# Low halves of the attention context made by adding transfers issued from GpSimd, in a perceiver block on one core

## The chip, the core and the metric

The kernel runs on one core of a Trainium2 chip. A core has a matrix engine (TensorE, called PE in the profile, with its weight loads under PEld), three elementwise engines (VectorE as DVE, ScalarE as ACT, GpSimd as POOL), a queue that issues the loads (SyncE as SP), and sixteen DMA engines behind the queues. The metric is the device time of one execution in microseconds. The kernel before took 231.92 us (median of 3 runs, 229.8 to 232.12).

## The reference

Two batch elements of 128 rows and 512 columns pass through three blocks, each added to `x`: a block of self-attention, cross-attention over a context of 2048 rows per batch element and a feed-forward; a recurrent block over two steps (the two batch elements); and an attention with selected experts. The change touches the first block:

```python
def self_attn(x, Wq, Wk, Wv):
    Q, K, V = (x @ Wq, x @ Wk, x @ Wv)
    energy = jnp.einsum('bqd,bkd->bqk', Q, K)      # masked by length and causally
    score = jax.nn.softmax(energy / np.sqrt(DK), axis=-1)
    return jnp.einsum('bqk,bkd->bqd', score, V)

def cross_attn(x, context, Wq, Wk, Wv):
    Q = x @ Wq
    K, V = (context @ Wk, context @ Wv)
    energy = jnp.einsum('bqd,bkd->bqk', Q, K)      # masked by length
    score = jax.nn.softmax(energy / np.sqrt(DK), axis=-1)
    return jnp.einsum('bqk,bkd->bqd', score, V)

z = self_attn(x, Wq1, Wk1, Wv1)
x = layer_norm(x + z, ln1_g, ln1_b)
z = cross_attn(x, context, Wq2, Wk2, Wv2)
x = layer_norm(x + z, ln2_g, ln2_b)
z = jax.nn.relu(x @ fc1_w + fc1_b) @ fc2_w + fc2_b
return layer_norm(x + z, ln3_g, ln3_b)
```

All inputs are float32. The kernel multiplies in another order: the scores are (x Wq2 Wk2^T) times the context, and the probabilities are multiplied with the context itself before Wv2.

## The kernel before

**Two ways to multiply.** A product of float32 operands is one call of the matrix engine that the profile shows as two matmul records. In the other way an operand is cut into a high half, rounded to the type fp32r, and a low half, what the rounding left over; the product is then three matmuls (high by high, high by low, low by high), one record each. The class `Halves` holds such a pair. `evac(dst, src)` makes it: ACT copies (CAST) into `dst.hi`, and DVE subtracts (TENSOR_TENSOR) `src - hi` into `dst.lo`.

**The context.** Each of the two batch elements (`t` = 0, 1) has its context in four groups `g` of 512 rows, twice: transposed (`ctxT`, tiles `cT`, for the scores) and as it is (`ctx`, tiles `cN`, for the products with the probabilities). A group is one load of 1 MB into a tile of 4 chunks. `load_ctxT` cuts all eight `cT` groups into halves. `load_ctxN` cuts only the groups in `PCR`, which are 0 and 1 of each batch element; groups 2 and 3 stay float32. I write cN02 for the group of `t` = 0, `g` = 2, and so on. `cross_attention` makes the scores of a group with 12 matmuls of 128x512, then counts, masks and takes the maximum (tiles `em`, `mx`, `nmax`, on DVE), the four exponentials (ACT, `em<-em,nmax`), turns each group of probabilities around on the matrix engine, copies it out of PSUM (`pT`), and adds the product with the context into one bank: 12 matmuls for a cut group, 4 for a whole one. The sum leaves as tile `PC`.

**Before the cross-attention.** `queries` normalises x, turns it (`hT`, halves) and multiplies with Wq1, Wk1, Wv1, each loaded in four chunks of 128 rows that `load_w` cuts into halves. `cross_queries` multiplies the turned result of the self-attention (`u1T`, float32) with Wq2 for both batch elements at once (128x256), and the result, in halves, with Wk2T.

**Memory.** Tiles of 8 KB per partition come from a pool with tag `wide` (8 of them, for loads and float32 weights) and a pool with tag `hl` (4 pairs, for halves). A tile's first writer waits until the last reader of the tile that had the place is done. The parameters, banks and small tiles have pools of their own.

**Order.** Nothing runs when the functions are called: `Program` and `Engine` number every operation in the order of the calls (line 172), and `emit(ORDER)` (line 158) issues them in an order written out by hand or by a tool, as numbers and runs such as `257+7`. Each engine takes its own instructions strictly in that order; an instruction that waits holds up all behind it on its engine. That is why all groups of the profile stand at line 161. In the kernel before the cross-attention's first exponential has number 642; just ahead of it on ACT stand the four copies of cN00.

Of the kernel before, what the change touches and what calls it, by code (L numbers as in the profile page):

```python
# [16 lines left out]
P = 128  # L17
# [25 lines left out]
257+7 0 249 1 250+1 4 2 275 7 252 3 276 20 17 26 423 277+1 23 253+2 35 38 256 29 32 279 281 18 280 265+4 10 271 21 272  # L43
283+1 446 19 285 22 291+1 282 293+1 317 287 24 27 273 288 286 270 295+1 318+2 289 25 28 321 274 297+2 322+1 290 300+3
324+1 30 304+1 33 306+2 343 309+2 326+1 312 328 313 44 344 39 36 329+3 31 345 333+1 34 335 346+4 314 40 37 336+2 351+5
339 357+9 340 88+1 424 41 5 369+7 45+1 90 42 57 367 91 377+10 315 43 50 11 388+4 316 95 395 426 409+2 368 464+1 396
412 427 92 8 341 47 51 393 413 115 52 394 342 414 48+1 61 466 397 62 467 398+1 415 468 9 428+1 400 430 469 431 63 401
473 432+1 470 93 435 434 416 471 67 417 58 472 418 402+1 436+4 419 474+1 420+1 476 404+2 441 477+1 94 96 442 407 443
79 484 444 408 445 479 447+2 481 422 450+1 480 53 485 482 486 483 487+1 453 452 454 489 455 490 492+1 491 496+1 68 456
494+1 458+1 64 498 457 80 86 461 499 460 81+1 84 87 85 59+1 54 65+1 69 83 120 70 122 121 116 512 502 513 503 514 504+3  # L50
515 508+1 516 510 517 550+1 518+1 522+2 552+1 525 511 526 554 520 527+1 555 529 556+1 521 558 530 559+2 531+1 562 118
533 563 534+2 564 537+3 123 541+2 565+1 544 567 545 119 500 568+2 546 117 571+2 547 604+3 71 608 574 609+3 578 613 501
73 72 575 591 614 97 548 759 615 579 77 74 78 133 576 75+1 580 592 581+1 593 583 577 584+2 594 587 616 98 588+1 617
595 102 549 103 596+1 154 100 99 598 618 599+1 619 104 101 620+1 106 138 136 12 601+1 134 105 785+1 622+3 16 139 425
183 137 590 626+1 142 140 135 107 787 628 788+4 746 109 747 603 124 141 760 108 761+1 110 629 113 630 111 15 13+1 198
631 112 125 127 632 763 793 764+5 748+1 770 750 128 639 637 129 131 635 640 55 772+1 126 774+1 794 776 795 751+1 777+2
633 753 796 638 157 646 636 159 161 634 155 641 130 642 651+1 754 653 643 654 780 114 755 669+1 756 132 655 657 671+1
163 166 174 156 781 658 757 158 656 645 659+1 782 661+2 783 160 164 673 664+1 162 666+1 165 668 167 674+1 644 687 676
696 677 688 697 689 678+1 168+1 680+2 690 56 170 784 698 683 699 758 173 186 171 771 797 172 190 175 177 188 798+1
684+2 691+1 145 181 146 179 800 178 693+2 803 700 807 801 805 143 804 808 701+2 802 806 809+1 819+2 180 811 144 822+1  # L60
704 825 176 837+1 826 705 707 824 827 708 828+2 706 711+1 839 831 184 709 715 812 840 832+1 813 147 238 182 716 185
864 717 865+1 834+2 841 843 867 814 189 199 187 844 842 718 710 855+1 719 857+1 720 713 194 815+2 845+5 151+1 200 193
148 647 149 648+1 721 851+1 722 191 150 723 153 724 192 714 859 725 462+1 213+1 868 853+1 726 743 195+1 215+1 860+2
217 197 225 219 863 650 727 869 729 870 730 728 731+1 218 871+1 733+2 226 937 739+1 220 240 221 736 204 873 227 874+2
879 737 877 234 880 913 925 883+1 878 738 914 885+1 881 887 741 915 742 882 888 916 889 917 890+1 990 205 744+1 206
235+1 892+1 918 894 201 818 202 926 895 897 896 898+1 919+4 927+5 934 900 924 203 938+3 933 209 942+1 935 231 901+1
944+2 903 936 911 947 904 912 905 948+1 210 950 906 952 951 907+1 910 978 909 232 979 966+4 228+1 971+2 980+2 974
983+1 975+1 985 987 986 988 991 953+3 992+2 957 960 958 961 959 962 977 995 963+2 222 996 989 997+2 1019 223 1020+1
1000 1022+1 1001+1 1179 1024 1029 1025 1031 230 1026 233 1005 1037+2 1003 1006 1076 1004 1084 1098 1030 1108 1099
1040+1 1102 1007 1027 212 1100 1032 1109 1078 1103 1085+1 1035 1033 239 1116 1110 1042 1120 1043 1101 1111 1044 1008+1  # L70
1013 1010 1014 1011+1 1015+1 237 1077 1017 1034 1117 1082 1119 224 1148 1018 1226 1045 1118 1036 1046 1151 1149+1 1228
1080 1227 1083 1047+1 1079 1087 1229+1 211 1054 1051 1231 1236 1232+2 1121 1088 1125+2 1104 1237 1105 1122+1 207 1050
1081 1112 1333 1313 1335 1089+5 1315 1314 1316+1 1290 1334 1332 1336 1343 1337 1095 1338 1344 1128 1339 1289 1287+1
208 1053 1055 1106 1056 1113 1291 1107 1292+1 1052 1049 1124 1096+1 1238 1355 1057 1129 1114+1 1356 1130 1132 1294+2
1345 1239 1065 1241 1062 1400 1028 1346 1297+3 1318 1340 1325 1301+1 1319 1326 1320+1 1240 1242 1133 1341 1354 1402
1401 1303+2 1243+1 1403 1327 1245+1 1328 1247 1353 1357 1071 1248 1347 6 1058+1 1131 1358+1 1363 1360 1364+2 1068 1361
1157 1249+7 1404 1060 1134 1061 1069 1342 1063+1 1322 1074 1306+1 1066 1073 1144 1308 1067 1158 1152+1 1070 1309 1142
1329 1351 1072 1348 1138 1154+1 1352 1075 1310 1141 1349 1139 1330 1145 1140 1136+1 1159+1 1198 1135 1367 1362 1146
1323 1331 1324 1147 1350 1173 1260 1259 1143 1311 1368 1162 1387 1370 1163 1263 1261 1371 1264 1262 1164 1156 1369
1258 243 1257 1161 1265 1269 1165 1267 1167+1 1405 1266 241 1268 1166 1271 1170+1 1406 1169 1273 1172 1372 245 1270  # L80
1378 1272 1388 1312 1384 1389 1278 1174+1 1276 1176 1180 1177 1181 1206 1182+1 1410+1 1385+1 1407 1412+1 1408 1390
1379 1277 1284 1281 1374 1391 1382 1280 1282 1285 1275 1392 1178 1286 1377 1279 1283 1394 1373 246 1376 1393 1184 1380
1395 1383 1375 1185 1396 1186+1 1397+1 1381 242 1188+1 244 1190+6 1207+2 248 1274 1197 1414 1409 1399 1415 1417 1416
1418+1 1210 1420 1199+3 1211 1429 1212 1421 1423 1422 1203 1213 1426 1204 1427+1 1424+1 1205 1214+2 1220 1217 1221
1218 1222 1219 1223+1 1454 1430+1 1435 1432+1 1436+2 1225 1483 1482 1439 1485+1 1484 1462 1487+2 1523 1532 1434 1440+2
1533 1490 1534 1443 1497+2 1444+3 1524 1450 1506 1500 1235 1448 1455 1451 1449 1453 1463 1452 1456 1464 1457 1465 1458
1466 1459+1 1467+1 1461 1469+3 1501+2 1491 1476 1473 1477 1474+1 1492 1507+1 1504 1535 1525 1478+1 1493 1526 1494 1509
1536 1510+1 1527+1 1537+1 1529 1512 1530 1539 1495 1480+1 1516 1612 1611 1496 1613+1 1521 1513 1617 1615 1505 1517
1531 1549 1540 1514 1550+2 1515 1569 1518 1570 1519 1571+1 1616 1618 1652 1620 1653 1621 1619 1622+1 1520 1522 1543
1553 1556 1554 1654 1562 1557 1555 1563 1661+4 1655 1545 1573 1577 1541+1 1574 1576 1635 1656+1 1575 1579 1582 1658+1  # L90
1636 1580 1559+1 1666 1544 1624 247 1625 1637 1626+2 1564 1629+1 1667 1638 1668 1650 1558 1583 1631+1 1581 1584 1639
1633 1660 1546 1640+2 1645 1644 1669 1646+1 1634 1643 1678+2 1561 1681 1578 1648 1698 1592 1699+1 1649 1651 1547 1672
1589 1673 1701 1670+1 1548 1585+3 1675+1 1682 1674 1683 1688 1565 1684 1686 1685 1689 1691+1 1702+1 1690 1677 1566
1687 1593 1567 1693 1718 1694+2 1704 1697 1705+1 1719 1708 1707 1709 1711+1 1710 1568 1714+1 1713 1716+1 1742+2 1733
1724+1 1720 1726+1 1721 1728+1 1722+1 1730 1734 1731 1735+1 1594 1745 1737+1 1732 1751 1746 1739+1 1747 1590+1 1741
1748 1756 1752 1595+1 1749 1597 1757 1598 1750 1599+1 1758 1753+1 1759+1 1755 1601 1606 1602+1 1607+1 1604+1 1609+1
"""
OPT = set("""psc fc2 Wv Wk u2col bfpe z4pe z1pe q2 hhcol""".split())

ON_ACT = [set("vsum vc vv bv".split()), set("vsum vc vv bv".split())]  # L100
PCR = [{0,1},{0,1}]
WHOLE = set("Wv1 Wv2 fc2 Wv Wk".split())
VPE = set()
WIDE_W = set("Wq1 Wk1".split())
NDUM, TDUM, HLB, WDB, UNS = 10, 0, 4, 8, 0


class Halves:
# [69 lines left out]
def perceiver_kernel(ctx: ExitStack, tc: tile.TileContext, a: dict, out: bass.AP):  # L178
# [81 lines left out]
    onemu = const.tile([P, 6 * KC], F32, name="onemu")  # L260


    def load(kind, dst, src):
        with program.on(kind):
            sync.dma_start(dst, src)

    class Rows:


        def __init__(self, name, n):  # L270
            self.tiles = []
            for i in range(0, n, 4):
# [13 lines left out]
    def load_w(name, n=C, rows=C):  # L286
# [13 lines left out]
        for k in range(kc):  # L300
            w = big.tile([P, C], F32, tag="stage", name=f"w_{name}", bufs=3) if whole is None else whole[:, k, :]
            load("s", w[:, :n], a[name][k * P : (k + 1) * P, :])
            with program.on("w"):
                evac(hl[:, k, :n], w[:, :n])
# [836 lines left out]
```

## Time and profile before

| | |
|---|---|
| median of 3 runs | 231.92 us (229.8 to 232.12) |
| the profiled execution | 230.57 us, of which the span of its instructions is 228.8 us |
| PE / DVE / ACT / POOL busy | 218.0 / 186.9 / 136.1 / 17.4 us |
| mean granted TensorE clock | 0.985 of full speed |
| moved by DMA | 43.41 MB, 190 GB/s on average |
| queries and self-attention | from the start to about 36 us |
| Wq2, Wk2T | 37.1 to 50.0 us |
| scores and products of the cross-attention | first scores at 49.98, last `PC` copy from 105.03 us |
| feed-forward, recurrent block, expert attention | from there to the end |

The page gives, for the most expensive groups of instructions, busy time, the mean duration of one, and what the engine waited for ahead of them. Consecutive instructions of an engine overlap a little at their ends, so what one costs in a row of them is the distance of the starts, which is worked out from the timeline: a row of n instructions that lasts L with a single duration d costs (L - d)/(n - 1) each. A matmul record of a float32 product is half of the product.

### The profile page before, as it was taken

Reading aid. Unit: us, or ns where it says so; the run is one execution under the profiler, and the core shown is the slowest. Engines: PE = TensorE matmul, PEld = TensorE weight load, DVE = VectorE, ACT = ScalarE, POOL = GpSimd, SP = SyncE. Lnnn points to the kernel's source line nnn. Section 1 sums busy time; section 2 is a strip of 40 time slices with the busy share of each in tenths; the row PEclk is TensorE's granted clock in tenths of the full one; section 3 lists DMA queues with packets and bytes.
Section 4 is the critical chain, followed back from the end, with each engine's and each line's share of the span. In section 5 each row is a group of like instructions: output and inputs, shape, how many; then the busy total and the mean of one; then the engine's idle time right before and its main releaser. Section 6 shows DMA issues by size and latency. Waiting matters only on the chain.

```text
span 228.8 us, 3607 instructions
## 1 busy us (share of the span) xinstructions
PE 218.0 (95%) x1186; PEld 179.8 (79%) x1186; DVE 186.9 (82%) x456; ACT 136.1 (59%) x418; POOL 17.4 (8%) x39
## 2 busy tenths in 40 slices
PE   7699997999999999999999999999999999998993
PEld 6499865898877846846898888888777978897992
DVE  4674588879999999978999769999997289999822
ACT  2766366727849939446569899988552316437020
POOL 3200001000000000001112200030302020000000
PEclk9999999999999999999999999999999999997699
DMA  5999799999653986858789600684050000000002
GB/s 178 329 393 335 235 370 392 320 322 341 201 221 116 365 299 218 315 151 327 264 294 409 239 0 3 197 288 158 0 209 0 0 1 3 0 1 3 0 0 92
DMA packets 21897, 43.41 MB, mean 190 GB/s; under 512 B 1283, under 2 KB 2871, under 8 KB 21879
## 3 DMA queue, kind: packets, MB, share of 16 engines
q1 hardware_dynamic: 21808, 43.16, 54.0%
q8 instruction: 9, 0.15, 0.3%
q14 instruction: 9, 0.07, 0.1%
q10 hardware_dynamic: 71, 0.03, 0.0%
HBM read 42.66 MB, written 0.52 MB: 189 GB/s over the span
## 4 chain that ended last, share of the span: by engine, by line
PE 58%; DVE 27%; ACT 5%; POOL 4%; DMA 2%; issue 2%; SPq 1%; DVEq 0%; POOLq 0%; ACTq 0%
PE bank L161 58%; DVE ve L161 4%; DVE st L161 3%; POOL rinv L161 2%; DMA w_Wq<-in_Wq_dram 2%; DVE Y L161 2%; DVE pr L161 2%; POOL rs L161 2%; ACT mix L161 2%; DVE X L161 1%; DVE nb L161 1%; DVE v L161 1%; SPq L161 1%; DVE mixhl L161 1%; DVE kn L161 1%
## 5 line engine op out<-in xcount | busy, mean ns | idle before, releaser
L161 DVE TENSOR_TENSOR hl_ctxT<-cT,hl_ctxT 128x512 fp32r<-128x512 f32 x32 | 20.8, 681 | 2.2 <-ACT hl_ctxT L161 2.1
L161 POOL TENSOR_TENSOR rinv<-ve,nhalf 128x1 f32<-128x1 f32 x16 | 10.6, 662 | 149.9 <-DVE ve L161 138.9
L161 ACT CAST hl_ctxT<-cT 128x512 fp32r<-128x512 f32 x32 | 18.2, 622 | 4.3 <-PE bank L161 2.5
L161 PE MATMUL bank<-hl_ctxT,qkTh 128*128 128x512 f32 x64 | 18.4, 394 | 0.0
L161 PE MATMUL bank<-cN,pT 128*128 128x512 f32 x32 | 14.5, 595 | 0.0
L161 PEld LDWEIGHTS bank<-hl_ctxT,qkTh 128*128 128x128 f32 x64 | 11.9, 188 | 2.3
L161 PE MATMUL bank<-hl_ctxN,pTh 128*128 128x512 f32 x32 | 11.9, 420 | 0.0
L161 DVE TENSOR_TENSOR hl_Wv<-w_Wv,hl_Wv 128x512 fp32r<-128x512 f32 x12 | 8.2, 688 | 4.1 <-ACT hl_Wv L161 4.1
L161 PE MATMUL bank<-hl_ctxT,qkTl 128*128 128x512 f32 x32 | 11.2, 396 | 0.0
L161 ACT CAST hl_ctxN<-cN 128x512 fp32r<-128x512 f32 x16 | 9.0, 619 | 3.1 <-PE bank L161 3.1
L161 PEld LDWEIGHTS bank<-cN,pT 128*128 128x128 f32 x32 | 5.9, 190 | 5.9 <-issue 5.7
L161 DVE TENSOR_TENSOR hl_ctxN<-cN,hl_ctxN 128x512 fp32r<-128x512 f32 x16 | 10.4, 681 | 0.0
L161 ACT CAST hl_Wv<-w_Wv 128x512 fp32r<-128x512 f32 x12 | 7.4, 625 | 4.7 <-DVE spread L161 3.4
L161 PE MATMUL bank<-xnT,w_fWk 128*128 128x128 f32 x64 | 9.8, 276 | 0.0
L161 PEld LDWEIGHTS bank<-xnT,w_fWk 128*128 128x128 f32 x64 | 8.7, 192 | 0.9
L161 PE MATMUL bank<-hT,hl_Wq 128*128 128x256 f32 x48 | 7.7, 293 | 1.8 <-ACT hT L161 1.8
L161 PE MATMUL bank<-xnT,w_fWq 128*128 128x128 f32 x64 | 9.3, 275 | 0.0
L161 PEld LDWEIGHTS bank<-xnT,w_fWq 128*128 128x128 f32 x64 | 8.4, 192 | 0.6
L161 PEld LDWEIGHTS bank<-u2T,w_fc 128*128 128x128 f32 x64 | 8.3, 191 | 0.7 <-ACT u2T L161 0.2
L161 PE MATMUL bank<-u2T,w_fc 128*128 128x128 f32 x64 | 8.8, 280 | 0.0
L161 PEld LDWEIGHTS bank<-hT,hl_Wq 128*128 128x128 f32 x48 | 6.5, 190 | 2.7 <-ACT hT L161 2.4
L161 PE MATMUL bank<-w_Wa,mix 128*128 128x256 f32 x32 | 8.5, 379 | 0.0
(282 smaller groups left out, 611.4 us busy)
## 6 DMA issues: line engine op xcount, KB each, us to landing
cT<-in_ctxT_dram SPq DMA_DIRECT2D x8, 1024.0 KB, 8.0
cN<-in_ctx_dram SPq DMA_DIRECT2D x8, 1024.0 KB, 5.5
spread<-in_spread_dram SPq DMA_DIRECT2D x9, 512.0 KB, 6.5
w_Wv<-in_Wv_dram SPq DMA_DIRECT2D x12, 256.0 KB, 3.5
w_Wk<-in_Wk_dram SPq DMA_DIRECT2D x8, 256.0 KB, 5.0
w_Wq<-in_Wq_dram SPq DMA_DIRECT2D x4, 256.0 KB, 4.6
w_Wq<-in_Wq_dram SPq DMA_DIRECT2D x1, 1024.0 KB, 9.4
w_Wk2T<-in_Wk2T_dram SPq DMA_DIRECT2D x4, 256.0 KB, 2.7
```

Source lines behind the costliest of these rows:

```text
L161: self.tc.keep_in_program_order(op(*args, **kwargs))
```

## The change

- `ACC = {"ctxN"}`: where a context group for the products is cut, DVE no longer makes the low half. ACT makes the high half as before, and also writes the negated high half into the place of the low one (`act.mul(..., -1.0)`, rounded to fp32r as well). Then one transfer from SBUF to SBUF, issued from GpSimd's queue, adds the float32 group onto it. Per group: 8 ACT instructions and 1 transfer of 1 MB in place of 4 ACT and 4 DVE instructions.
- `PCR` goes from groups {0,1} and {0,1} to {0,1,2} and {0,1,2,3}: 7 of 8 groups are cut instead of 4. Only cN03 stays float32.
- `MIX = {"Wq1": 1}`: the first chunk of Wq1 is not cut. It is multiplied as float32 with a float32 copy of the first chunk of the turned x (`hF`, two extra ACT copies); the other three chunks as before.
- `q2row`: the product with Wq2 is made for one batch element at a time (128x128 instead of 128x256, twice as many).
- One pool: halves are two tiles of the tag `wide`, which has 16 places; the tag `hl` is gone.
- The two small loads of `turn_rows` move from ACT's queue into the numbered program, on SP.
- `TAILW` adds matmuls that keep the matrix engine busy at the end; all its counts are 0, so it adds none.
- A new `ORDER`. The number of an operation changes where operations are added ahead of it: the load of cN02 is now 174, its four high halves 175, 177, 179, 181, its four negated copies 176, 178, 180, 182, its adding transfer 183, and the first exponential is 687. The load of cN00 is 154, of cN01 164, of cN11 195; the tile cT11 is loaded by 115 and cut by 116 to 123.

```diff
-OPT = set("""psc fc2 Wv Wk u2col bfpe z4pe z1pe q2 hhcol""".split())
+OPT = set("""psc fc2 Wv Wk u2col bfpe z4pe z1pe q2 hhcol q2row""".split())
-PCR = [{0,1},{0,1}]
+PCR = [{0,1,2},{0,1,2,3}]
+MIX = {"Wq1": 1}
+ACC = {"ctxN"}
+TAILW = (0, 0, 0)
-    big = ctx.enter_context(tc.tile_pool(name="big", bufs=8))
+    big = ctx.enter_context(tc.tile_pool(name="big", bufs=16))
...
     def halves(name):
-        hl = big.tile([P, 2, KC, C], F32R, tag="hl", name=f"hl_{name}", bufs=4)
-        return Halves(hl[:, 0], hl[:, 1])
+        return Halves(*(big.tile([P, KC, C], F32R, tag="wide", name=f"hl_{name}") for _ in range(2)))
+
+    def cut(hl, w, n, acc):
+        for k in range(n):
+            if acc:
+                act.copy(hl.hi[:, k, :], w[:, k, :])
+                act.mul(hl.lo[:, k, :], w[:, k, :], -1.0)
+            else:
+                evac(hl[:, k, :], w[:, k, :])
+        if acc:
+            pool.dma_start(hl.lo, w, accum_op=ALU.add)
...
             load("s", w[:, :n], a[name][k * P : (k + 1) * P, :])
+            if k < MIX.get(name, 0):
+                continue
             with program.on("w"):
                 evac(hl[:, k, :n], w[:, :n])
+        if name in MIX:
+            W[name, "whole"] = whole
...
+                m = slice((j + i) * P, (j + i + 1) * P)
+                for kc in range(nw):
+                    pe.matmul(po[:, i, :], whole[:, kc, m], xF[:, kc, :], start=kc == 0, stop=False)
+                matmuls(po[:, i, :], [(w[:, kc, m], xT[:, kc, :]) for kc in range(nw, KC)], False, begun=nw > 0)
...
                 ctxN[t, g] = hl = halves("ctxN")
                 with program.on("w"):
-                    for j in range(4):
-                        evac(hl[:, j, :], c[:, j, :])
+                    cut(hl, c, KC, "ctxN" in ACC)
...
-            for m, po in project_turned(u1T, W["Wq2"], T * P):
-                evac(qT[:, m, :], po)
+            if "q2row" in OPT:
+                for t in range(T):
+                    for m, po in project_turned(u1T[:, :, token(t)], W["Wq2"]):
+                        evac(qT[:, m, token(t)], po)
```

The part of the new `ORDER` around the cutting of cN02 and the first exponential:

```diff
+155 168 121 166 123 170 12 14 172 13 681 15 165 194 167 683 163 803 820 850 804 821+1 805 823 806 824 807 174 180 173
+178 195 679 686 176 808 182 838 851 175 825 809+3 687 696+2 16 852+1 690 750 688 699+1 751+2 714 689 701 715 205 854
```

## Prediction

> **What bounds it.** I read the page's busy line and the chain first.
>
> ```profile
> span 228.8 us, 3607 instructions
> PE 218.0 (95%) x1186; PEld 179.8 (79%) x1186; DVE 186.9 (82%) x456; ACT 136.1 (59%) x418; POOL 17.4 (8%) x39
> ...
> PE 58%; DVE 27%; ACT 5%; POOL 4%; DMA 2%; issue 2%; SPq 1%; DVEq 0%; POOLq 0%; ACTq 0%
> ```
>
> The matrix engine is busy 218.0 of 228.8 us, so work taken from it is worth its time, and any hole made in it costs its length. Next, the ten-microsecond stretches of the cross-attention (busy time of PE, PEld, DVE, ACT, POOL; clock; DMA share; GB/s):
>
> ```profile
> 50.00:60.00 10.00, 10.00 (x47) 8.26 (x46) 9.90 (x21) 7.64 (x16) 0.00 (x0) 1.00 0.76 271
> 60.00:70.00 10.00, 10.00 (x45) 8.09 (x44) 9.90 (x28) 6.58 (x13) 0.00 (x0) 1.00 0.63 224
> 70.00:80.00 10.00, 10.00 (x52) 7.83 (x52) 9.97 (x22) 9.49 (x22) 0.00 (x0) 1.00 0.79 272
> 80.00:90.00 10.00, 10.00 (x37) 5.12 (x35) 9.24 (x23) 6.05 (x15) 0.00 (x0) 1.00 0.66 238
> 90.00:100.00 10.00, 10.00 (x46) 7.38 (x45) 8.72 (x22) 5.79 (x14) 0.00 (x0) 1.00 0.76 280
> ```
>
> PE has no hole, DVE almost none, ACT has a third free. The change loads the free one. Unit prices come from rows without a hole in the timeline (start, length, engine, what, count, idle before):
>
> ```profile
> 62.49 1.75 PE L161 MATMUL bank<-hl_ctxT,qkTh 128*128 128x512 f32 x7
> 81.12 5.42 PE L161 MATMUL bank<-cN,pT 128*128 128x512 f32 x12
> 37.14 6.31 PE L161 MATMUL bank<-u1T,w_Wq 128*128 128x256 f32 x28
> 115.88 3.99 PE L161 MATMUL bank<-u2T,w_fc 128*128 128x128 f32 x32
> 19.12 3.04 PE L161 MATMUL bank<-hT,hl_Wk 128*128 128x256 f32 x24
> 35.64 1.56 PE L161 MATMUL bank<-ident,x 128*128 128x128 f32 x8 [1.86 <-DVE x L161]
> 74.94 3.74 ACT L161 CAST hl_ctxN<-cN 128x512 fp32r<-128x512 f32 x7
> 90.25 1.28 DVE L161 TENSOR_TENSOR hl_ctxN<-cN,hl_ctxN 128x512 fp32r<-128x512 f32 x2
> ```
>
> With the single durations of the groups (0.39, 0.59, 0.38, 0.27, 0.28; ACT 0.62; DVE 0.68) a halved 128x512 matmul costs 0.227 us, a float32 record 0.439 (a product has two), float32 at 256 columns 0.220, at 128 columns 0.120, halved at 256 columns 0.120, an ACT copy 0.52, a DVE subtraction 0.60.
>
> **Part by part.** *Three more groups cut:* 12 products of 0.878 become 36 matmuls of 0.227: 10.5 to 8.2, PE gains 2.3 us, all on the path. DVE gets three more subtractions for the probabilities, 1.8, but loses sixteen for cN, 9.6.
>
> *Negated copies:* ACT makes 56 copies for cN instead of 16, 40 x 0.52 = 20.8 us more. I take the multiplying copy at the plain copy's price; at the distance of the exponentials (0.73 with their sum) it would be up to 0.2 x 28 = 5.6 more. From the last copy of the combined queries (x Wq2 Wk2T, about the first scores) the new order gives ACT until the `PC` of the second batch element: 13 copies for cT and 52 for cN (33.8), 8 exponentials (5.8), 8 copies of probabilities at 0.49 (3.9), 7 weight copies (3.6), small ones 2.6: 49.7 us. PE has in this stage 96 score matmuls (21.8), 84 halved products (19.1), 8 float32 records (3.5), 12 for Wv2 (2.7), some 5 of turning and first fc1: 52. ACT goes from two thirds to 95% of the stage. It fits only if it never waits.
>
> *It waits.* In a pool of n places I give the k-th tile of `ORDER` (by first write) the place that is freed as number k - n (by last read). That this holds is shown by the kernel before: the pair of cN00 is the 13th of 4 places and gets the 9th freed, the first cT group of the second batch element that the scores are done with, and ACT stood for it:
>
> ```profile
> 67.30 2.19 ACT L161 CAST hl_ctxN<-cN 128x512 fp32r<-128x512 f32 x4 [3.11 <-PE bank L161]
> ```
>
> In the one pool of 16, cN02 is the 45th tile and gets the place freed as 29th: cT11, whose last reader is DVE's subtraction 123. Counting from the first scores, s = 49.98 in this trace, DVE has ahead of it, itself included, 19 subtractions (11.4), 4 counts (2.4), length and masks (2.1), one maximum (0.6), two query halves (1.0): 17.5 without a wait. But cT11 and cT13 are themselves loaded into places that Wk2T and the first scores free, at s and s+3, 5 us before they land, and the low half of cT10 gets a place when the third group's scores end, at s+9; such waits make it up to 21. On SP the load of cN02 stands behind cN01 alone, which is early. It then takes 5.1 at least:
>
> ```profile
> cN<-in_ctx_dram SPq DMA_DIRECT2D x8, 1024.0 KB, 5.5
> ...
> DMA to landing us min/median/max: 5.1/5.5/14.4
> ```
>
> so cN02 is there at s+22.6 to s+26. ACT has come to it by s+20 and holds up all behind it. Its copies 180, 178, 176, 182, 175 stand ahead of exponential 687 there: five, 2.6 us. The first exponential begins at s+25.2 to s+28.7; in the trace before it began at 69.71, s+19.7, on the maximum alone. After it come two more, the copy of the probabilities and its low half, 3.3, then the first product, at s+28.5 to s+32. PE is through its 96 scores at s+22 and has 12 transposes, 1.5, so it stands 5 to 8.4 us. What follows is 29 us for PE and 31 for ACT from the first exponential (29 copies for cN 15.1, weights 3.6, the rest above), so the second `PC` comes at s+57 to s+61 against 105.03 - 49.98 = s+55: 2 to 6 later, the 2.3 already spent. I take 4.
>
> *Transfers.* No row shows an adding transfer. It reads two tiles and writes one, so from below it is a plain 1 MB load, 5.1 to landing; from above the slowest such load, 14.4. I take about 8, nearer the median. Between the last negated copy and the first use the new order leaves 10 to 11 us for cN01, cN02, cN11, cN12, cN13: it decides above that. On the engines, 43.16 MB took 54% of the span, 2.9 us per MB; seven transfers at once or twice that are 20 to 40 us, while 50 to 100 us has 14 free (the DMA column). The overflow of 6 to 26 us moves loads back; the weights of the recurrent block can take it (130 to 140 us has a DMA share of 0.01), the groups of the context can't, so I put it into the rival of late transfers. The Trainium skill, "DMA: Bandwidth & Descriptors", Rules for kernel authors, says the same against the change: another issuing queue gives no bandwidth, all run on the same 16 engines. Its section on the anatomy of one DMA fits 2.0 us plus bytes/436e3, an estimate of 4.4 for 1 MB from GpSimd; by it the transfers would never be late, and the sum would be the one above. On GpSimd's queue the normalisation `x0 rinv` stands behind the transfer of cN13, which waits for ACT's copies; it is early by some 5 us.
>
> *Front.* Wq2 by row: 64 x 0.120 = 7.7 for 32 x 0.220 = 7.0, +0.7; the 1.86 us hole ahead of the turned x shrinks, as the second element's work can lie under Wq2 of the first: I leave 0.5, so -1.4. First chunk whole: 8 x 0.220 for 12 x 0.120, +0.3; one copy (0.52) leaves the start, two of 128x128 come in: 0. Sum -0.4, from -0.9 to +1. `turn_rows`: needed late, 0; on SP it stands behind cT00, two issues of 0.4 us. The pool by itself: as many bytes as before, 0 beyond the waits above; `TAILW`: 0.
>
> *Behind.* Nine weight chunks are still to be cut after the second `PC` instead of six: three subtractions, 1.8, where DVE is busy 0.96 and 0.91 of the two stretches from 110 us. 0 to 1.8; I take 0.8.
>
> Sum: 230.57 (this execution) + 4 - 0.4 + 0.8 = **235.0**. The profiled execution lies 1.35 below the median 231.92, within the spread of the runs (1%), about what a measurement can tell from no change.
>
> **Rivals.** *Faster:* the place of cN02 is free sooner than by my count. To leave no hole the first exponential must begin by s+20.3, so cN02 must land by s+17.7 and be issued by s+12.6. Then PE's 2.3 stays gained, with up to 0.9 in front: 227.4 to 229.6, say 228. For it speaks that DVE is relieved by 7.8 and that ACT's sum fits; against it the order on ACT and the load's 5.1. At the end 5 us ran at half clock (210 to 215); another order could give 2.5 either way. *Transfers late:* if they take 14.4 instead of 10, each batch element's first tight group costs 4.4 more: 235 + 8.8 = 244. *Nothing:* DVE's relief is worth nothing since PE is the bound, ACT's waits eat PE's 2.3: 231.
>
> **Numbers.** Forecast 0.52 (232.5 to 239.4: 2 to 6, front up to +1, behind up to 1.8), late transfers 0.12 (239.4 to 248), faster 0.27 (226.5 to 229.6), nothing 0.09 (229.6 to 232.5). Range 227 to 241, leaving out about 0.05 below and 0.08 above. Faster by over 1% (below 229.6): 0.27; slower (above 234.2): 0.12 and 0.43 of the forecast, 0.55; within: 0.18.
>
> **What would show it.** Right: a hole in PE of 5 us or more just ahead of the first products with the context, ACT waiting there for the load of cN02, DVE well under 9 in the stretches from 50 to 100, 84 halved and 8 float32 records. Wrong: the first exponential within 21 us of the first scores and no hole; or adding transfers landing later than 10 us after their issue, with waits on them; or a Wq2 stage that still begins behind a hole of 1.9 us.

## The result, and the profile after

The changed kernel takes **257.98 us** (median of 4 runs, 255.63 to 259.67), the kernel before on the same chip 230.86 (228.34 to 232.12): a ratio of 1.123, 95% interval 1.105 to 1.141. The forecast was 235.0, with a range up to 241. The direction was right and the size was not: 27 us are lost where 4 were expected. (Some executions of every kernel show a lower granted clock and are over 1.5% longer; ratios here, and times and ratios of the experiments below, leave these out, and the number of runs left is given where it is one or two; the changed kernel then takes 257.3.)

The page of the changed kernel first: busy times, two rows of the 40 slices, the two DMA queues that matter (q1 carries the loads, q0 what GpSimd issues), and the chain that ended last by engine.

```profile
span 253.7 us, 3743 instructions
...
PE 221.5 (87%) x1226; PEld 186.8 (74%) x1226; DVE 180.4 (71%) x444; ACT 156.4 (62%) x461; POOL 23.1 (9%) x46
...
PEclk9999999999995589997968999999999999999799
DMA  6989972999399999999994889992000000000002
...
q1 hardware_dynamic: 21879, 43.19, 47.6%
q0 software_dynamic: 1008, 7.34, 14.4%
...
PE 58%; DMA 18%; DVE 11%; ACT 7%; issue 2%; POOL 1%; SPq 1%; POOLq 0%; ACTq 0%; DVEq 0%
```

PE is no longer busy 95% of the span but 87%. The chain holds 18% DMA where it held 2%. The DMA row is full (9) in all slices but one from 44 to 133 us, which before it was not, and the clock falls to a half in two slices. The seven adding transfers moved 7.34 MB and took 14.4% of the engines' 253.7 us, 36.5 us: 5.2 us of all sixteen engines for one transfer of 1 MB. The loads took 120.8 us for 43.19 MB, 2.8 per MB. **An added megabyte costs the engines nearly twice a loaded one.**

The same stretches that the prediction showed, with the later ones (busy time of PE, PEld, DVE, ACT, POOL; clock; DMA share; GB/s):

```profile
70.00:80.00 10.00, 3.45 (x16) 2.52 (x14) 4.50 (x17) 0.28 (x1) 0.52 (x2) 0.85 1.01 227
80.00:90.00 10.00, 3.79 (x15) 3.17 (x16) 1.43 (x3) 7.18 (x17) 0.87 (x1) 0.50 1.03 357
...
110.00:120.00 10.00, 6.48 (x24) 4.59 (x23) 5.65 (x13) 4.96 (x10) 0.56 (x1) 0.90 1.04 236
120.00:130.00 10.00, 4.88 (x20) 3.17 (x19) 1.08 (x2) 1.73 (x4) 0.00 (x0) 0.84 1.03 386
```

There are two holes, 70 to 90 and 110 to 130 us, and in both every engine but the DMA engines is idle for a part. What ACT and PE wait for is seen in their timelines (start, length, engine, operation, idle before and what ended it):

```profile
69.15 1.12 ACT L166 CAST hl_ctxN<-cN 128x512 fp32r<-128x512 f32 x2
82.75 2.19 ACT L166 ACTIVATE hl_ctxN<-cN 128x512 fp32r<-128x512 f32 x4 [12.47 <-DMA cN<-in_ctx_dram]
...
85.35 0.72 ACT L166 ACTIVATE em<-em,nmax 128x512 f32<-128x512 f32 x1
...
128.27 1.14 ACT L166 CAST hl_fc<-w_fc 128x512 fp32r<-128x512 f32 x2 [13.31 <-DMA w_fc<-in_fc_dram]
```

```profile
86.21 2.46 PE L166 MATMUL bank<-ident,em 128*128 128x128 f32 x10 [12.77 <-ACT em L166]
...
129.82 1.22 PE L166 MATMUL bank<-u2T,w_fc 128*128 128x128 f32 x4 [4.09 <-ACT u2T L166]
```

The first hole is the one of the prediction: ACT stands for the load of cN02, with the first exponential queued behind its copies, and PE stands for the exponential. But it is 12.8 us long, not 5 to 8, and it lies ahead of the turning of the probabilities, since that needs the exponentials. The second was not in the prediction: ACT stands 13.3 us for a chunk of fc2, whose load was issued at 109.78 us and took 18.5, and behind it are the turned `u2T` and the second `PC`. Three more waits of PE between the two are for adding transfers themselves: 0.87, 2.65 and 1.03 us, for cN11, cN12 and cN13.

Where the 25.06 us between the two profiled executions (255.63 and 230.57) come from:

| stretch | before | after | difference |
|---|---|---|---|
| start to first scores | 49.98 | 47.60 | -2.4 |
| first scores to second `PC` | 55.05 | 83.90 | +28.85 |
| second `PC` to the end of the span | 123.8 | 122.2 | -1.6 |
| outside the span | 1.77 | 1.93 | +0.2 |

In the middle stretch PE was busy all of its 55.05 us before. Now it is busy 59.52 of 83.90 and stands 24.38, which is the sum of seven waits: 1.80 and 1.17 (behind cT groups that landed late), 12.77, the three of the transfers, and 4.09. Its busy time is not 2.3 shorter but 4.5 longer. Some 1.1 of that is work that has only moved: six records of products with `u2T` and two more transposes of `x` stand ahead of the second `PC` (6 x 0.12 + 2 x 0.18), and the next stretch lacks them. The rest has two reasons in the same rows, which I have not separated: the clock, 0.88 on average here against 1.00, and rows of matmuls broken up by waits, in which each counts its whole duration.

What the DMA engines did while cN02 was on its way (67.8, its issue, to 82.7; packets, MB, share of the engines, then the landing time of the loads issued in that window):

```profile
q0 software_dynamic: 288, 2.10, 75.2%
q1 hardware_dynamic: 718, 1.44, 27.3%
...
cN<-in_ctx_dram SPq DMA_DIRECT2D x4, 1024.0 KB, 14.9
```

Two adding transfers, those of cN00 (issued at 66.43) and cN01 (69.54), took three quarters of the engines' time in this window; 1.44 MB of loads had the rest (cN02 and a part of what was issued behind it). cN02 was issued at s + 20.2 (s is the time of the first scores), inside the s + 17.5 to 21 of the prediction, and landed 14.9 us later, where the prediction took 5.1.

### The profile page after: what moved, and what is told of

The parts are those of the page before. It is cut to its first block, busy times and chain, and to the rows that moved or that the text cites. A ratio compares the mean times of both kernels' runs of the same rounds, so it can differ in the third digit from the quotient of the medians.

```text
span 253.7 us, 3743 instructions
## 1 busy us (share of the span) xinstructions
PE 221.5 (87%) x1226; PEld 186.8 (74%) x1226; DVE 180.4 (71%) x444; ACT 156.4 (62%) x461; POOL 23.1 (9%) x46
## 3 DMA queue, kind: packets, MB, share of 16 engines
q1 hardware_dynamic: 21879, 43.19, 47.6%
q0 software_dynamic: 1008, 7.34, 14.4%
## 4 chain that ended last, share of the span: by engine, by line
PE 58%; DMA 18%; DVE 11%; ACT 7%; issue 2%; POOL 1%; SPq 1%; POOLq 0%; ACTq 0%; DVEq 0%
PE bank L166 58%; DMA w_fc<-in_fc_dram 7%; DMA cN<-in_ctx_dram 6%; DMA cT<-in_ctxT_dram 4%; DVE ve L166 3%; ACT hl_ctxN L166 3%; DMA w_Wq<-in_Wq_dram 1%; DVE Y L166 1%; ACT em L166 1%; DVE nb L166 1%; DVE hl_ctxT L166 1%; ACT u2T L166 1%; DVE st L166 1%; POOL rinv L166 1%; ACT hl_ctxT L166 1%
## 5 line engine op out<-in xcount | busy, mean ns | idle before, releaser
L166 PE MATMUL bank<-hl_ctxN,pTh 128*128 128x512 f32 x56 | 21.8, 454 | 4.5 <-DMA hl_ctxN<-cN 4.5
L166 ACT ACTIVATE hl_ctxN<-cN 128x512 fp32r<-128x512 f32 x28 | 16.2, 624 | 12.9 <-DMA cN<-in_ctx_dram 12.9
L166 PE MATMUL bank<-ident,em 128*128 128x128 f32 x34 | 7.9, 331 | 12.8 <-ACT em L166 12.8
L166 PEld LDWEIGHTS bank<-hl_ctxN,pTh 128*128 128x128 f32 x56 | 11.4, 208 | 9.1 <-DMA hl_ctxN<-cN 5.9
L166 DVE TENSOR_TENSOR pTl<-bank,pTh 128x512 fp32r<-128x512 f32 x7 | 4.8, 687 | 17.6 <-ACT pTh L166 17.6
L166 PEld LDWEIGHTS bank<-ident,em 128*128 128x128 f32 x34 | 5.1, 167 | 15.5 <-ACT em L166 14.0
L166 ACT CAST hl_ctxN<-cN 128x512 fp32r<-128x512 f32 x28 | 15.7, 624 | 0.2 <-DVE hl_ctxT L166 0.2
L166 PEld LDWEIGHTS bank<-hl_ctxT,qkTh 128*128 128x128 f32 x64 | 11.8, 188 | 4.6 <-ACT hl_ctxT L166 2.2
L166 PE MATMUL bank<-hl_ctxN,pTl 128*128 128x512 f32 x28 | 12.5, 446 | 0.0
L166 POOL DMA_DIRECT2D hl_ctxN<-cN x7 | 6.3, 899 | 63.7 <-ACT hl_ctxN L166 49.0
L166 DVE TENSOR_TENSOR hl_fc<-w_fc,hl_fc 128x512 fp32r<-128x512 f32 x4 | 2.7, 688 | 12.2 <-ACT hl_fc L166 12.2
L166 ACT CAST hl_fc<-w_fc 128x512 fp32r<-128x512 f32 x4 | 2.4, 618 | 13.3 <-DMA w_fc<-in_fc_dram 13.3
## 6 DMA issues: line engine op xcount, KB each, us to landing
hl_ctxN<-cN POOLq DMA_DIRECT2D x7, 1024.0 KB, 11.8
```

The costliest lines, as they stand in the source:

```text
L166: self.tc.keep_in_program_order(op(*args, **kwargs))
```

## The experiments

All start from the changed kernel unless another is named. Where an experiment leaves low halves incomplete, its time is read for the order of events alone.

**The transfers without their bytes.** Eight columns of 2048 are added; every copy, wait, place and number of the order stays.

```diff
-            pool.dma_start(hl.lo, w, accum_op=ALU.add)
+            pool.dma_start(hl.lo[:, 0, 0:8], w[:, 0, 0:8], accum_op=ALU.add)
```

> The changed kernel, with each adding transfer cut down to 8 of its 2048 columns; the copies on ACT, the order, the pool and the waits stay. The low halves are left wrong but for those 8 columns, so the output is not the reference's. Theory (the transfers fill the DMA engines and make the loads late): with 7.3 MB gone from the engines the load of cN02 lands in about 5.5 us instead of 14.9, fc2's chunks arrive before ACT comes to them, and what is left is the hole of the prediction: 232 to 240 us. Rival (order and places): the loads are issued late because their places come free late, whatever the transfers do; the holes stay and the time is 250 us or more. Rival (ACT has 40 more copies to make): they are still here, so it stays at 245 or more.

Measured: 229.01 us in the one run left (all four: 229.01 to 234.85); the kernel before has 227.22 to 230.56. With the bytes alone, 28 us are gone, or 24 by the median of all four (233.89). The profiled execution took 234.33 us at a granted clock of 0.963. ACT waits for cN02 and PE for the exponential, but briefly (the load of cN02 first, then ACT, then PE):

```profile
63.88 4.99 DMA cN<-in_ctx_dram
...
68.95 2.19 ACT L166 ACTIVATE hl_ctxN<-cN 128x512 fp32r<-128x512 f32 x4 [1.97 <-DMA cN<-in_ctx_dram]
...
72.42 0.55 PE L166 MATMUL bank<-ident,em 128*128 128x128 f32 x3 [2.20 <-ACT em L166]
```

The rival of ACT's 40 more copies falls: they are all here. So does the rival of order and places as the cause of the large loss: both are unchanged. What they cost by themselves isn't settled: in the profiled execution the second `PC` comes at s + 57.9, against s + 55.05 before, but at a granted clock of 0.97 in this stage against 1.00, and with the 1.1 us of moved work in it; the one run of 229.0 is no longer than the kernel before.

This run also splits what the transfers did to cN02. Here its load was issued at s + 16.2 (63.88 - 47.70) and landed after 5.0 us; in the changed kernel at s + 20.2 and after 14.9. So of the 13.9 us by which cN02 came later, 9.9 are its own flight and 4.0 its issue. The issue waits for DVE to be done with cT11. In the changed kernel the loads of cT11 and cT13 were issued beside the transfer of cN10 (42.3 to 54.1 us) and took 8.9 and 9.9 us, and DVE stood 2.9 us for cT13; with tiny transfers cT11's took 5.1 and DVE did not stand.

**Half of the bytes, and the bytes without the adding.**

```diff
-            pool.dma_start(hl.lo, w, accum_op=ALU.add)
+            pool.dma_start(hl.lo[:, 0:2, :], w[:, 0:2, :], accum_op=ALU.add)
```

> The changed kernel, with each adding transfer moving two of its four chunks (0.5 MB); all else stays. Half of each low half is left wrong, so the output is not the reference's. Theory of the transfers: in between, 240 to 250 us, with the load of cN02 landing in 8 to 12 us. Rivals of order and of ACT's load: as the whole transfer, 253 to 259.

```diff
-            pool.dma_start(hl.lo, w, accum_op=ALU.add)
+            pool.dma_start(hl.lo, w)
```

> The changed kernel with each adding transfer as a plain copy of the same 1 MB from tile to tile (the low halves are then the whole values, so the output is not the reference's); order, copies and waits stay. If the adding makes them dear (5.2 against 2.8 us of the engines for a plain MB), this gives 235 to 244, as the half transfers did (236), since the engine time is about halved. If moving 7.3 MB more is dear in itself: 250 to 259.

Measured: 236.1 us with the halves (ratio 1.029, 1.014 to 1.043), 238.1 with plain copies of all bytes (two runs; 1.042, 1.030 to 1.054). With the changed kernel and the tiny transfers this is a row of four. The two waits follow the time that q0 takes from the engines (its share times the span), not the bytes:

| transfers | MB moved by q0 | engines' time of q0 | PE's first hole | ACT's first wait for fc2 | time |
|---|---|---|---|---|---|
| 8 columns | 0.03 | 1.6 us | 2.2 | 1.1 | 229.0 (one run) |
| half, adding | 3.67 | 20.4 | 5.8 | 5.4 | 236.1 |
| whole, plain | 7.34 | 19.0 | 5.6 | 6.3 | 238.1 |
| whole, adding | 7.34 | 36.5 | 12.8 | 13.3 | 257.3 |

The halves came out below what was expected (240 to 250): the first 19 to 20 us of transfers cost 7 to 9, the next 16 to 18 cost 19 to 21. Up to there the gaps of the engines take more than half of it.

**The price by itself.** Behind the kernel before, on idle DMA engines, one tile of 1 MB is moved again and again from GpSimd.

```diff
+    pool.dma_start(src, given)
+    pool.dma_start(other, given)
+    pool.dma_start(dst, src)
+    pool.dma_start(dst, src, accum_op=ALU.add)
+    pool.dma_start(dst, src, accum_op=ALU.add)
+    pool.dma_start(dst, other)
+    pool.dma_start(dst, src, accum_op=ALU.add)
+    sync.dma_start(other, given)
```

> The kernel before, and behind it, on the otherwise idle DMA engines, transfers of one 1 MB tile one after the other from GpSimd: two plain loads from HBM, a plain SBUF to SBUF copy, two adding transfers, a plain copy, then an adding transfer beside a plain load from SyncE. The total time has no meaning (it is longer by these). Theory: an adding transfer costs the engines about 5 us by itself and lands in 7 to 9, a plain copy or load in 4.5 to 6; beside a load both take longer, 8 to 11. Rival (it was only contention): alone, the adding transfer lands in 5 to 6 like the others.

The DMA view of the window 217 to 224.1 us, with the first adding transfer alone (share of the engines; landing time), then of 232 to 236.5, with the second plain copy:

```profile
q0 software_dynamic: 144, 1.05, 73.0%
...
hl_pc<-pa POOLq DMA_DIRECT2D x1, 1024.0 KB, 7.0
```

```profile
q0 software_dynamic: 144, 1.05, 60.5%
...
hl_pc<-pb POOLq DMA_DIRECT2D x1, 1024.0 KB, 4.2
```

Alone, the adding transfer lands 7.0 us after its issue (the second, beside stores of the output, 7.3) and takes 0.730 x 7.1 = 5.2 us of the engines; the plain copy 4.2 and 0.605 x 4.5 = 2.7 (the first plain copy, issued while a load was still on its way, 6.1). Beside a load from SyncE the adding one took 10.9 and the load 6.2. So the rival, that it was only contention, falls: the price is there on idle engines.

**Which transfers make which hole.** The first three (cN10, cN00, cN01) or the last four (cN02, cN11, cN12, cN13) are cut to 8 columns, the others stay whole. `t == 0 and g < 2 or g == 0` names the first three; in the second kernel the condition is negated.

```diff
+            m = slice(0, 8) if t == 0 and g < 2 or g == 0 else slice(0, KC * C)
-            pool.dma_start(hl.lo, w, accum_op=ALU.add)
+            pool.dma_start(hl.lo.rearrange("p k c -> p (k c)")[:, m], w.rearrange("p k c -> p (k c)")[:, m], accum_op=ALU.add)
```

> The changed kernel with the first three adding transfers (cN10, cN00, cN01) cut to 8 columns and the last four whole; everything else as in the change (the low halves of the three are wrong but for 8 columns, so the output is not the reference's). Local theory (a load waits for the transfers that stand on the engines just then): the hole ahead of the turned probabilities is 2 to 3 us as with tiny transfers, the wait for fc2's chunks stays near 13; 243 to 249. Theory of the sum (only the engine time of the whole stage counts; three transfers fewer are 15 us less): both holes shrink, 238 to 242.

> The converse: the first three whole, the last four cut to 8 columns (their low halves wrong but for these). Local theory: the hole ahead of the turned probabilities is 11 to 13 us as in the changed kernel, the wait for fc2's chunks below 3; 243 to 249, and what the two runs lie above 234 adds up to about the 24 us of the changed kernel. Theory of the sum: 238 to 244, both holes there and smaller.

Measured: 242.7 us with the last four whole (ratio 1.051, 1.042 to 1.059), 243.59 with the first three (one run; all four: 243.59 to 249.87). The load of cN02, two of PE's waits and ACT's wait for fc2 with the last four:

```profile
63.59 4.94 DMA cN<-in_ctx_dram
...
72.08 0.55 PE L166 MATMUL bank<-ident,em 128*128 128x128 f32 x3 [2.19 <-ACT em L166]
...
116.49 1.22 PE L166 MATMUL bank<-u2T,w_fc 128*128 128x128 f32 x4 [4.24 <-ACT u2T L166]
...
114.94 1.14 ACT L166 CAST hl_fc<-w_fc 128x512 fp32r<-128x512 f32 x2 [13.59 <-DMA w_fc<-in_fc_dram]
```

and the same with the first three, where PE has no wait for `u2T`:

```profile
67.99 14.97 DMA cN<-in_ctx_dram
...
86.51 2.46 PE L166 MATMUL bank<-ident,em 128*128 128x128 f32 x10 [12.89 <-ACT em L166]
...
125.41 0.62 ACT L166 CAST hl_fc<-w_fc 128x512 fp32r<-128x512 f32 x1 [2.93 <-DMA w_fc<-in_fc_dram]
```

With the last four the load of cN02 takes 4.9 us, the first hole is that of the tiny transfers (2.19), and ACT waits 13.59 us for fc2, as in the changed kernel. With the first three the load takes 15.0, the first hole is whole (12.89), and ACT waits for fc2 2.9 us at most. Above 229.0 they lie 13.7 and 14.6, together 28.3; the changed kernel lies 28.2 above (two of these times are single runs). **The local theory holds:** what counts is not the engines' time summed over the stage, but which load is issued while a transfer stands on the engines, and who waits for that load.

**Three transfers, the rest by DVE.** The output is complete here.

```diff
-                    cut(hl, c, KC, "ctxN" in ACC)
+                    cut(hl, c, KC, (t, g) in ((1, 0), (0, 0), (0, 1)))
```

> The changed kernel with adding transfers for the first three cut groups alone (cN10, cN00, cN01); the other four have their low halves from DVE again. All seven groups are cut and the output is complete. Theory (the engines have room for some 14 to 20 us of transfers, not for 36): three take 15 us, so loads land nearly as with half transfers, and DVE has 9.6 us more than in the changed kernel: 234 to 241. Rival (each whole transfer lands late whatever the others do, since it takes 7 us alone and 11 beside a load): 245 to 252.

Measured: 247.2 us (ratio 1.080, 1.073 to 1.087), the rival's number. I had expected the three to find room, by the sum. This miss led to the two runs above: PE's first hole is 10.9 us here too, and ACT's wait for fc2 is 0.3.

**All low halves by DVE**, in the order of the change (`ACC` empty; the seven transfers and the negated copies are gone).

```diff
-ACC = {"ctxN"}
+ACC = set()
```

> The changed kernel with the low halves made by DVE's subtraction as before: no negated copies, no adding transfers; seven groups cut, the new order, the one pool and the front stay. Theory of the transfers: 230 to 240, DVE busy near 197 us, ACT near 142. Rival of ACT's load: the same, so only together with the run of the tiny transfers does this tell the two apart. Rival of order and places: 250 or more here too.

Measured: 239.7 us (ratio 1.044, 1.033 to 1.055), at the upper end of the first theory, with DVE busy 196.3 and ACT 142.5 us as expected. Without a single transfer the seven cut groups are no gain either in this order. DVE is busy 9.86 of each ten microseconds from 60 to 80, where PE has holes, and from 60 to 70 the DMA engines are almost idle; ACT stands for the load of cN02 here too, 8.6 us:

```profile
60.00:70.00 10.00, 7.32 (x25) 5.29 (x24) 9.86 (x25) 2.86 (x6) 0.00 (x0) 0.83 0.16 53
70.00:80.00 10.00, 7.93 (x40) 5.87 (x39) 9.86 (x27) 5.50 (x14) 0.00 (x0) 1.00 0.91 332
```

**Another order on ACT**, first with whole transfers, then with tiny ones. The numbers are ACT's alone, with others left out between them; the subtractions on DVE that follow fc2's casts move with them.

```diff
-180 178 176 182 175 ... 687 690 688 700 689
+687 690 688 700 689 180 178 176 182 175
...
-233 227 791 792 795 236 796 945 946 949 953
+791 792 795 796 945 946 949 953 233 227 236
```

> The changed kernel, transfers whole, with two moves in the order of ACT: the first five copies for cN02 go behind the four exponentials and the first copy of probabilities, and the casts of fc2's chunks 2, 0, 3 go behind the second PC and its halves. Theory: the two holes of 12.8 and 13 us come from waits at the head of ACT's queue, so they shrink, but the transfers still land in 8 to 17 us and the products wait for them instead: 240 to 250. Rival (the waits on ACT are all there is, and transfers and loads would be in time for the matrix engine): 228 to 236. Rival (nothing is gained, each wait moves to the next instruction): 253 to 259.

> The changed kernel with the transfers cut to 8 columns (low halves wrong but for these) and, besides, the five copies for cN02 behind the exponentials and fc2's casts behind the second PC. With the tiny transfers alone there were left a hole of 2.2 us ahead of the turned probabilities, with ACT waiting for the load of cN02, and one of 1.1 to 2.9 for fc2. If the forecast's mechanism (the load of cN02 at the head of ACT's queue) is right, the first hole goes here and the second PC comes 2 to 3 us earlier: 229 to 232. Rival (PE then waits for the low halves of cN00 and cN01 or for DVE instead): the same as with tiny transfers alone, 233 to 235.

Measured with whole transfers: 256.1 us (ratio 1.120, 1.105 to 1.136). Nothing is gained beyond the spread of the runs, against my theory and for the last rival. The first exponential began at 72.33 instead of 85.35, and PE stood again as soon as it came to the products:

```profile
88.12 1.22 PE L166 MATMUL bank<-hl_ctxN,pTh 128*128 128x512 f32 x2 [8.33 <-ACT pTh L166]
96.84 0.80 PE L166 MATMUL bank<-hl_ctxN,pTh 128*128 128x512 f32 x1 [2.79 <-DMA hl_ctxN<-cN]
```

ACT now stands for cN02 one step later (7.1 us, before the copy of the second group's probabilities), and PE then waits for the transfer of cN02 itself. With tiny transfers: 232.0 us (ratio 1.015, 1.008 to 1.022). The first exponential began at s + 20.7, waiting for its maximum alone, and no hole stands ahead of the turned probabilities. So the wait that the prediction built on, the load of cN02 at the head of ACT's queue, is shown. What it is worth isn't: the second `PC` comes at s + 56.3 instead of 57.9, but the granted clock in the stage was 1.00 against 0.97, PE has a new wait of 1.13 us before the first products, and the moved casts of fc2 made one of 3.9 us before fc2's products. The time, 232.0, is not below the 229.0 of the tiny transfers alone.

**The transfers in the kernel before**: its order, its two pools and four cut groups, each negated copy right behind its high half, each transfer behind the last of its group. The lines are against the changed kernel; the pools and the order are those of the kernel before.

```diff
-OPT = set("""psc fc2 Wv Wk u2col bfpe z4pe z1pe q2 hhcol q2row""".split())
+OPT = set("""psc fc2 Wv Wk u2col bfpe z4pe z1pe q2 hhcol""".split())
-PCR = [{0,1,2},{0,1,2,3}]
+PCR = [{0,1},{0,1}]
-MIX = {"Wq1": 1}
+MIX = {}
```

> The kernel before, its order, its pools and its four cut groups, with the low halves of these four made as in the change: 16 negated copies on ACT right behind the high ones, 4 adding transfers, 16 subtractions less on DVE. Theory (the transfers take the DMA engines): four of them at 5.2 us of all engines are 21 us more, where 50 to 100 us had 14 free; loads and low halves come late and PE waits: 236 to 246. Rival (the new order and the pool are what made the waits, the transfers only in that order): DVE's relief of 9.6 us is worth little, ACT has room, 228 to 232.

Measured: 262.3 us (two runs; ratio 1.148, 1.134 to 1.161), outside both expectations and worse than the change, with only four transfers. In this order the cuts stand shortly before their use, and PE waits 7 to 10 us for each of three transfers:

```profile
85.63 0.79 PE L164 MATMUL bank<-hl_ctxN,pTh 128*128 128x512 f32 x1 [9.73 <-DMA hl_ctxN<-cN]
101.49 0.77 PE L164 MATMUL bank<-hl_ctxN,pTh 128*128 128x512 f32 x1 [6.95 <-DMA hl_ctxN<-cN]
126.79 0.79 PE L164 MATMUL bank<-hl_ctxN,pTh 128*128 128x512 f32 x1 [8.64 <-DMA hl_ctxN<-cN]
```

Part of the products of cN01 are issued ahead of its transfer here and use the negated copy, so the low half of that group is incomplete, and the transfer waits for those products. The run says what the change's order does: it gives the transfers a lead and hides most of their own length. PE waits 25.3 us for the four here, and 4.5 for the seven of the changed kernel.

**The front by itself**, on the kernel before: both parts, the whole Wq1 chunk alone, and both parts with the cuts of hT01 and Wk2T put between the two batch elements.

```diff
+MIX = {"Wq1": 1}
+OPT = set("""... q2row""".split())
```

> The kernel before with the two front parts of the change alone: first Wq1 chunk whole, and the product with Wq2 for one batch element at a time, its order kept but for these. No adding transfers, four groups cut, the pools of before. In the changed kernel the first scores began at 47.60 instead of 49.98 us. If these two parts made that gain, the first scores begin 1.5 to 2.5 us earlier and the time is 228 to 229.5, faster by about 1%. Rival: the gain is of the new order and the later loads, and here it is 0.4 or less: 230 to 231.

> The kernel before with one part of the change alone: the first chunk of Wq1 whole, multiplied as float32. In the kernel before PE stood 1.78 us ahead of the first Wq1 product (9.43 us); in the changed kernel it begins at 8.05. If this part stands by itself: the first Wq1 product 1.2 to 1.5 us earlier, PE 0.3 more busy, so the first scores about 1 us earlier and 229 to 230 us. Rival (the gain is eaten by the next wait, such as the load of the other chunks): first scores within 0.3 of 49.98 and no change, 230.5 to 231.5.

> The kernel before with the two front parts (first Wq1 chunk whole, Wq2 for one batch element at a time), with the cuts of hT01 and Wk2T placed between the turned x of the two elements, where the first try had ACT wait behind them. In that try PE stood 1.86 us ahead of the turned x, 0.33 and 2.79 behind. If the parts made the 2.4 us that the changed kernel gains in front, the first scores begin at 47.6 to 48.8 and the time is 228 to 230. Rival (the gain came from the new order of the self-attention and the later loads): first scores at 49 to 51, 230 to 232.

Measured: 232.0 (ratio 1.015, 1.006 to 1.023), 231.45 (1.012, 1.006 to 1.018) and 230.8 us (1.006, 0.997 to 1.014); first scores at 54.3, 50.4 and 52.0 us, where the changed kernel has 47.6 and the kernel before 49.98. None is faster, the first two are slower by about 1%; the gains that I had expected of the parts did not come. With the whole chunk alone the first product of Wq1 does begin earlier, at 8.65 instead of 9.43, and then PE stands 1.30 us at 11.55 for the second half of the turned x. In both runs with Wq2 by element the 1.86 us hole ahead of the turned x is still there. So the 2.4 us that the changed kernel gains in front are not the two parts by themselves in the order of before; which step of the new order makes them I have not tested. What the trace shows is where they come from: ahead of the first scores PE stands 2.9 us in the changed kernel and 5.7 before. The 1.86 us hole is gone, and the 1.78 us ahead of the first Wq1 product are 0.15.

No version that was run is faster than the kernel before by more than the spread of the runs.

## Why the prediction was right or wrong

- **What bounds it: right.** PE was the bound, and holes in it cost their length: the seven holes sum to 24.38 of the 28.85 us.
- **Three more groups, -2.3: consistent.** With tiny transfers and the exponentials first, PE is busy 216.8 us against 218.0 before; by the prediction's own terms, 218.0 - 2.3 + 0.7 + 0.3 = 216.7.
- **Negated copies, +20.8 on ACT: right.** ACT is busy 156.4 against 136.1, +20.3; four multiplying copies take 2.19, as four plain ones did. ACT "fits only if it never waits" was the right warning.
- **It waits: the place and the queue were right, the price of the load was not.** This is the step that failed. ACT stood for cN02, and the exponential stood behind. But "it then takes 5.1 at least" was used as its price, and the load took 14.9, since the transfers of cN00 and cN01, which the new order starts at that very time, took 75% of the engines. Without the bytes of the first three transfers it took 4.9 (last four whole) and 5.0 (all tiny).
- **That the issue fell inside its forecast is luck.** It came at s + 20.2 (forecast 17.5 to 21), but without the bytes of the first three transfers at s + 16.2: the count of DVE's work was at least 1.3 us too long, and the transfers made up for it.
- **The 4 us of the sum are not shown.** With tiny transfers the first exponential began at s + 23.9 (25.2 to 28.7) and the hole was 2.4 (5 to 8.4), less than half of the least forecast. The second `PC` at s + 57.9 lies in the forecast (57 to 61), but at a granted clock of 0.97 in the stage; at 1.00, with the other order on ACT, it came at s + 56.3. The one run of 229.0 is no longer than the kernel before, where the sum gave 235.0.
- **Transfers: the total was right, and the sum put it at nothing.** Seven transfers were to take 20 to 40 us of the engines and took 36.5, with 14 free. But the overflow was put on loads that "can take it", and its price into a rival with a chance of 0.12; the loads next in the queue were cN02 and fc2's chunks, and they could not. To landing I took about 8; they took 8.3 to 17.1, median 11.8, and 7.0 alone, with waits on them, which was one of the named signs of being wrong. That rival was too small as well (244): it priced the products' own waits, 4.4 for one group of each element, and they came to 0.87 + 2.65 + 1.03 = 4.55 for three groups of the second, so the like number is chance. The prediction read the DMA share of whole stretches; the runs with three and four whole transfers show that the loss goes by what is issued beside what.
- **The second hole was not priced at all.** fc2's loads were issued from 104.5 us, beside the transfers of cN11, cN12 and cN13 (100.1 to 105.7), and ACT's order has their casts ahead of `u2T` and the second `PC`. The four last transfers are worth 13.7 us (242.7 against 229.0), through it and through the products' waits for them.
- **What a hole costs besides its length was left out.** Over the middle stretch PE is busy 59.52 us for what would be 55.05 - 2.3 + 1.1 of moved work = 53.8 in the unbroken rows and at the clock of before: 5.7 us, a fifth of the loss, beside the holes themselves. With tiny transfers and the other order on ACT, at a granted clock of 1.00 in the stage, it is 54.5.
- **Front, -0.4: too small**; it was -2.4, and not by the two parts named: the hole of 1.86, of which 0.5 was left standing, went whole, and so did most of the 1.78 ahead of the first Wq1 product. **Behind, +0.8: not decided.** It was -1.6, of which 1.1 is the work that moved ahead of the second `PC`; with tiny transfers, the same order and the same work, the stretch took 127.0 us in place of 122.2. `x0 rinv` behind the transfer of cN13, which I held to be early enough, was: it began at 113.81, after a wait for DVE, 8 us behind that transfer's issue.

The prediction named a rule that spoke against the change and put nothing into the sum for it. The Trainium skill, "DMA: Bandwidth & Descriptors", Rules for kernel authors, says that another issuing queue gives no bandwidth, all run on the same 16 engines. The window above is that rule in numbers, 75.2% and 27.3% of one set of engines. The estimate of 4.4 us that I worked out from its section on the anatomy of one DMA holds here for the plain copy on idle engines (4.2) and not for the adding transfer (7.0): that section speaks of moving bytes, not of adding them.

## What to carry to other kernels

A transfer that looks free because its queue is idle is paid in the loads that are issued beside it. List what else is issued in the 10 us behind each transfer, and who stands first in line for that. A mean DMA share of ten microseconds, such as the 0.76 of the kernel before, does not answer this: what is free in it need not be free when the one urgent load is issued. When a wait for a load stands at the head of an engine's queue, price the load at what it takes beside everything that the change adds, not at its median.

## What the runs showed of the hardware that I had not expected

- An adding transfer from SBUF to SBUF takes 5.2 us of all DMA engines for 1 MB, a plain copy 2.7, and 7.0 against 4.2 us to landing, on idle engines. Its half tiles cost more per byte: 20.4 us for 3.67 MB, against 36.5 for 7.34, both in the changed kernel.
- Issuing was held up too while the adding transfers stood on the engines. The duration of the instructions on SP's queue that issue fc1 and fc2 (minimum, median, maximum in ns), in the changed kernel and then in the kernel before:

```profile
L166 SPq DMA_DIRECT2D w_fc<-in_fc_dram x5: 337/712/7021, 104.5 to 129.6; - x5
```

```profile
L161 SPq DMA_DIRECT2D w_fc<-in_fc_dram x5: 327/341/871, 48.9 to 106.3; - x5
```

  One issue took 7.0 us, with all that SP has to issue behind it; it is the fc2 chunk that ACT waits for. With the last four transfers whole the longest took 8.1 us, with them cut to 8 columns 0.46.
- Around the PE hole of 12.8 us (73.4 to 86.2) the granted clock was 0.85 from 70 to 80, 0.50 from 80 to 90 and 0.97 in the next ten.
